# Rounding of the activations on ScalarE, tap sums in PSUM tiles of their own, and a later flag sum in the end of a cross-attention and feed-forward kernel

## The chip, the cores and the metric

The kernel runs on one core of a Trainium2 chip. The time is device microseconds of one execution, as the median of several runs; lower is better. A core has five engines with a queue each, worked in order: TensorE (PE, with its weight loads shown as PEld), VectorE (DVE), ScalarE (ACT), GpSimd (POOL) and SyncE (SP), which mostly issues DMAs. They wait for each other through semaphores.

## The reference

One layer: latents x (2048 x 256) attend to 1601 context rows and to themselves with 4 heads of 64; then comes a feed-forward part with weights rounded to -1, 0, 1 and activations rounded to 8 bits. What matters here is the second part:

```
xq = round(layernorm(x) * 127/max) / (127/max)         # per token
h  = xq @ w1q.T                                        # 256 -> 1024
h  = conv along the tokens, 3 taps, one filter per channel, plus conv_b
h  = silu(h)
hq = round(h * 127/max) / (127/max)                    # per token, max over the 1024 channels
x  = x + hq @ w2q.T                                    # 1024 -> 256
```

## The kernel before

Attention comes first and takes some 590 us: eight units (512 queries x a pair of heads), each with 30 blocks of 128 keys. Scores, an exponential on ScalarE and the product with the values follow each other in a software pipeline; denominators are summed by VectorE and by adding DMAs. It uses an estimate of the row maxima, and a flag (`behind`) says in the end whether the estimate was good enough; only if not, the whole layer is run a second time (`tc.If` in the last lines; this does not happen here).

The feed-forward part works on groups of 256 tokens (8 groups, `NG`), with the 1024 channels as partitions: 8 chunks of 128 channels, two chunks to a "slot", four slots to a group. Groups 0 to 3 are planned into the beats of the attention loop by a table of due times (`plan`, `at`). Group 4's first slot too. The rest runs after the loop: slots 17 to 31 (groups 4 to 7), written out by hand in `tick(i)`, together with the end of attention for the last four blocks of 128 tokens (`head(i)`) and what is left of group 3 (`rest`: its scale rows, its two roundings and its two products, one a tick). All instructions issued through `tensor`, `vector`, `scalar` and `gpsimd` keep the order in which the Python code issues them.

A slot in this last stage goes like this (names as in the profile):

- `hidden`: TensorE, four matmuls into a two-bank PSUM tile `ph` (both chunks, 258 tokens: one more on each side).
- `dequantize`: VectorE multiplies `ph` by the row of token scales `ib_all` into `h` in SBUF.
- first chunk: `end_convolve`, three matmuls with diagonal matrices `dg`, one per tap (six records in the profile), whose sum goes back into the first bank of the slot's `ph`; then ScalarE's Silu with `cb_sb` as bias (`end_silu(s, 0)`) into `t`.
- second chunk: `end_taps`, two ScalarE passes into `pre` and `side`; `end_last_tap`, VectorE adds the third tap into `pre` and GpSimd adds `side`; then Silu (`end_silu(s, 1)`) into `t`.

`t` is 256 tokens x 4 channels of one half group (two slots), with tokens outermost, so a Silu writes one 4-byte value in every 16 bytes.

At the end of a group's slots VectorE takes the maximum over the channels of a half (`magnitudes`, `m`), TensorE transposes it (`tpa`), VectorE makes scales (`am`, `qsc`), GpSimd (ScalarE for the last group) spreads them over a tile `cm`, TensorE transposes that (`tpb`), and ScalarE copies it to `tb`. Then for each half `rounding`: VectorE multiplies `t` by `tb` in place, and rounds by adding and subtracting a large constant (`MAGIC`) in one instruction (line 953), into `hq` in bf16 (one buffer), 4 channels in every 8. `product` is TensorE's eight matmuls `py` per 128 tokens, the first four from half 0 of `hq`, the next four from half 1; two such products make a group. `output` is VectorE's `res` and a DMA to `out` on SyncE's queue; it runs one tick later, ahead of that tick's remaining VectorE work.

[...] In the last stage `ps_1` holds one (transposes), `ph` two tiles of two banks, and `ps_y` three single banks (`dn`, `po`, `py`, `many`). So a `hidden` waits until the Silu of the slot two before has read its sum out of the same tile.

`flag` (line 1134): after the last group's scales VectorE compares the last denominators (`within`, `near`, `worst`), TensorE sums over the partitions (`many`), and VectorE copies the sum to `behind`. TensorE's `tpb` for the last group is issued behind `many`.

Of the kernel before, what the change touches and what calls it, by code (L numbers as in the profile page):

```python
# [10 lines left out]
F32 = mybir.dt.float32  # L11
# [3 lines left out]
AF = mybir.ActivationFunctionType  # L15
ALU = mybir.AluOpType
AX = mybir.AxisListType
PSUM = bass.MemoryType.PSUM

P = 128  # L20
FMAX = 3.4028234663852886e38
MAGIC = 12582912.0
# [7 lines left out]
def layer(  # L30
# [22 lines left out]
    nc = tc.nc  # L53
# [10 lines left out]
    G = 256  # L64
    QPG = G // P
    NG = NL // G
    QW = 512
# [15 lines left out]
    const = ctx.enter_context(tc.tile_pool(name="const", bufs=1))  # L83
# [7 lines left out]
    ones = const.tile([P, P], F32, name="ones")  # L91
    nc.gpsimd.memset(ones, 1.0)
    ones16 = const.tile([P, P], BF16, name="ones16")
    nc.vector.memset(ones16, 1.0)

    neg_half = const.tile([P, 2 * H], F32, name="neg_half")
    nc.gpsimd.memset(neg_half, -0.5)

# [13 lines left out]
    cb_sb = const.tile([P, NH], F32, name="cb_sb")  # L112
# [27 lines left out]
    att = ExitStack()  # L140
# [12 lines left out]
    def big(name):  # L153
        return ps_b.tile([P, 2, 512], F32, tag="big", name=name)
# [19 lines left out]
    tensor, vector = InOrder(nc.tensor), InOrder(nc.vector)  # L174
    scalar, gpsimd = InOrder(nc.scalar), InOrder(nc.gpsimd)
# [108 lines left out]
    with tc.tile_pool(name="pro", bufs=1, side="right") as pro, tc.tile_pool(  # L284
        name="pw", bufs=2, side="right"
# [3 lines left out]
        for a in range(0, NX, 512):  # L289
            n = min(512, NX - a)  # L290
# [338 lines left out]
    with att:  # L629
# [89 lines left out]
        def compare(u, r):  # L719

            if behind is None:
                return
            within = wk.tile([P, QW], BF16, tag="within", name="within")
            vector.tensor_scalar(within, r, math.exp(LAG), None, ALU.is_le)
            vector.scalar_tensor_tensor(within, r, math.exp(-LAG), within, ALU.is_ge, ALU.mult)
            vector.tensor_reduce(near[:, u : u + 1], within, AX.X, ALU.min)
# [72 lines left out]
        for edge in (0, NL + 1):  # L799
# [3 lines left out]
        NC2 = NH // 2  # L803
        groups_ = [{} for _ in range(NG)]
        chunk = {}
        where = {
            "ph": big, "py": lambda: big("py")[:, 0, :D], "later": False,
            "t": lambda: fp.tile([P, G, NC2], F32, tag="t", name="t", bufs=3),
        }
# [12 lines left out]
        def dequantize(s):  # L822
            t0 = s // NP * G
            h = fp.tile([P, 2, G + 2], F32, tag="h", name="h", bufs=2)
            vector.tensor_tensor(
                h, chunk[s]["ph"][:, :, : G + 2],
                ib_all[:, t0 : t0 + G + 2].unsqueeze(1).to_broadcast([P, 2, G + 2]), ALU.mult,
            )
            chunk[s]["h"] = h
# [56 lines left out]

        def end_convolve(s):
            c = s % NP * 2
            for tap in range(3):
                tensor.matmul(  # L890
                    chunk[s]["ph"][:, 0, :G], chunk[c, tap], chunk[s]["h"][:, 0, tap : G + tap],
                    start=(tap == 0), stop=(tap == 2),
                )

        def end_last_tap(s):
            c = s % NP * 2
            h, pre, side = chunk[s]["h"], chunk[s]["pre"], chunk[s]["side"]
            vector.scalar_tensor_tensor(
                pre[:, 1, :], h[:, 1, 2 : G + 2], cw_sb[:, c + 1, 2:3], pre[:, 1, :],
                ALU.mult, ALU.add,  # L900
            )
            gpsimd.tensor_tensor(pre[:, 1, :], pre[:, 1, :], side[:, 1, :], ALU.add)

        def end_silu(s, j):
            g, c = s // NP, s % NP * 2
            if c % NC2 == 0 and j == 0:
                groups_[g].setdefault("t", []).append(where["t"]())
            t = groups_[g]["t"][c // NC2][:, :, c % NC2 + j]
            if j == 0:
                scalar.activation(t, chunk[s]["ph"][:, 0, :G], AF.Silu, bias=cb_sb[:, c : c + 1])  # L910
            else:
                scalar.activation(t, chunk.pop(s)["pre"][:, 1, :], AF.Silu)

# [31 lines left out]
        def rounding(g, i, tokens=slice(0, G)):  # L945
            b = groups_[g]
            t = b["t"][i][:, tokens, :]
            vector.tensor_tensor(
                t, t, b["tb"][:, tokens].unsqueeze(2).to_broadcast(list(t.shape)), ALU.mult
            )  # L950
            if "hq" not in b:
                b["hq"] = fp.tile([P, G, NH], BF16, tag="hq", name="hq", bufs=1)
            vector.tensor_scalar(
                b["hq"][:, tokens, ts(i, NC2)], t, MAGIC, -MAGIC, ALU.add, ALU.add
            )

        def product(g, i):
            b = groups_[g]
            py = b["py", i] = where["py"]()
            for c in range(NH):  # L960
                tensor.matmul(
                    py, b["hq"][:, ts(i, P), c], w2T[:, c, :], start=(c == 0), stop=(c == NH - 1)
                )
# [45 lines left out]
        def unit_beat(k):  # L1009

            u, b = divmod(k, NB)
            return (u, b, beats[b]) if u < len(units) else (u, b, [])
# [11 lines left out]
        for k in range(len(units) * NB):  # L1024
            u, b, blocks = unit_beat(k)
            v, _, following = unit_beat(k + 1)
            g, pr = units[u]
# [49 lines left out]


        loop_ps.close()
        ps_h = att.enter_context(tc.tile_pool(name="ps_h", bufs=2, space=PSUM))  # L1080
        ps_y = att.enter_context(tc.tile_pool(name="ps_y", bufs=3, space=PSUM))

        def y_bank(name):
            return ps_y.tile([P, QW], F32, tag="y", name=name)

        where.update(
            ph=lambda name: ps_h.tile([P, 2, 512], F32, tag="ph", name=name),
            py=lambda: y_bank("py")[:, :D],
            later=True,
            t=lambda: ptp.tile([P, 2, QW], F32, tag="pt", name="t").rearrange(  # L1090
                "p h q -> p (h q)"
            ).rearrange("p (t c) -> p t c", c=NC2),
# [22 lines left out]
        def run(sub, *names):  # L1115
            for n in names:
                steps[sub][n]()
# [16 lines left out]
        def flag():  # L1134

            compare(len(units) - 1, r)
            if behind is None:
                return
            worst = sm.tile([P, 1], F32, tag="worst", name="worst")
            vector.tensor_reduce(worst, near, AX.X, ALU.min)  # L1140
            vector.tensor_scalar(worst, worst, 0.5, None, ALU.is_lt)
            many = y_bank("many")[:, :1]
            tensor.matmul(many, ones, worst, start=True, stop=True)
            vector.tensor_copy(behind, many)

        rest = [call for key in sorted(plan) for call in plan.pop(key)]
        slots = list(range(4 * NP + 1, NG * NP))
        N = len(slots)

        def tick(i):  # L1150

            at_ = {i - ((g - 4) * NP - 1) + (g == NG - 1): g for g in range(4, NG)}
            if 0 <= i - 2 < N:
                end_silu(slots[i - 2], 1)
            if 0 <= i - 1 < N:
                end_silu(slots[i - 1], 0)
            if i < N:
                dequantize(slots[i])
            if i >= N and 0 <= i - 1 < N:
                end_last_tap(slots[i - 1])  # L1160
            if 6 in at_:
                magnitudes(at_[6], 1)
                columns(at_[6])
            while outputs:
                output(*outputs.pop(0))
            if 0 <= i - 1 < N and i < N:
                end_last_tap(slots[i - 1])
            if i < N:
                end_taps(slots[i])
            if 6 in at_:  # L1170
                scales(at_[6], at_[6] == NG - 1)
                if at_[6] == NG - 1:
                    flag()
            if 7 in at_ and at_[7] != NG - 1:
                scales_spread(at_[7])
                rounding(at_[7], 0)
            if 8 in at_ and at_[8] != NG - 1:
                rounding(at_[8], 1)
            if 4 in at_:
                magnitudes(at_[4], 0)  # L1180
            if 7 in at_ and at_[7] == NG - 1:
                g = at_[7]
                scales_spread(g, True)
                for n in range(QPG):
                    for half in range(2):
                        rounding(g, half, ts(n, P))
                    product(g, n)
                for n in range(QPG):
                    output(g, n)
            if i + 1 < N:  # L1190
                hidden(slots[i + 1])
            if i < N:
                end_convolve(slots[i])
            if 1 <= i <= NSUB:
                run(i - 1, TURN)
            if 8 in at_ and at_[8] != NG - 1:
                for n in range(QPG):
                    end_product(at_[8], n)
# [54 lines left out]
```

## Time and profile before

| | us |
|---|---|
| median of 3 runs | 688.37 (687.83 to 688.69) |
| the profiled execution | 688.55 |
| its span, first to last instruction | 686.7 |
| TensorE busy | 629.2 (92%) |
| VectorE busy | 464.1 (68%) |
| ScalarE busy | 423.8 (62%) |
| GpSimd busy | 276.6 (40%) |
| last row of VectorE (res) starts | 681.89 |

The profile is of one execution. Rows of the timeline show the start within the span, the duration, the engine and operation, the output and inputs, and in brackets how long the engine had been idle and who ended it. Most instructions are recorded in a helper, so that all have the line of that helper (L170), and one goes by tile names. The granted clock is the share of full speed that TensorE was given; over the whole span it is 0.972, and all that is missing is missing in the last 70 us.

### The profile page before, as it was taken

How to read it: one execution, taken by the hardware profiler on the slowest of the kernel's cores; microseconds unless marked ns; L12 is line 12 of the kernel's file. 1: busy time of each engine (PE TensorE's matmuls, PEld its weight loads, DVE VectorE, ACT ScalarE, POOL GpSimd, SP SyncE). 2: the span in 40 equal slices, each digit the busy share in tenths (PEclk: the TensorE clock that was granted, in tenths of full speed). 3: DMA queues.
4: the chain of work that ended last, by engine and by line, in shares of the span. 5: the costliest groups of instructions: out<-in, count | busy, mean ns of one | idle time of the engine just before them, and what ended most of it. 6: DMA issues, size and time to landing. Idle time of an engine off the chain costs nothing. (4 is left out here: it accounts for less than half of the span.)

```text
span 686.7 us, 8000 instructions
## 1 busy us (share of the span) xinstructions
PE 629.2 (92%) x2796; PEld 266.3 (39%) x2796; DVE 464.1 (68%) x770; ACT 423.8 (62%) x535; POOL 276.6 (40%) x331
## 2 busy tenths in 40 slices
PE   4999898999999999999999999998899999857754
PEld 2555563333333333333334333332333333345542
DVE  3658774332832766596378779757966797897885
ACT  1656556554556445669945469998765789545540
POOL 2656673221221234244245433425354446742330
PEclk9999999999999999999999999999999999997975
DMA  7600003685878674478849447693564576100001
GB/s 241 170 0 0 1 1 92 128 161 111 167 140 183 128 148 93 93 154 152 185 96 172 101 107 154 125 182 94 107 123 92 132 138 114 31 0 16 16 16 36
DMA packets 32220, 72.12 MB, mean 105 GB/s; under 512 B 7531, under 2 KB 16940, under 8 KB 32172
## 3 DMA queue, kind: packets, MB, share of 16 engines
q0 software_dynamic: 16560, 60.30, 43.3%
q1 hardware_dynamic: 14524, 10.45, 5.1%
q10 hardware_dynamic: 1088, 0.79, 0.4%
q8 instruction: 24, 0.39, 0.2%
q14 instruction: 24, 0.20, 0.1%
HBM read 9.13 MB, written 2.10 MB: 16 GB/s over the span
## 5 line engine op out<-in xcount | busy, mean ns | idle before, releaser
L170 ACT ACTIVATE pt<-st,bias 128x1024 f32<-128x1024 f32 x232 | 242.8, 1112 | 123.1 <-issue 64.6
L170 PE MATMUL st<-q_un,kT 64*128 64x512 f32 x928 | 223.7, 611 | 4.7 <-DVE res L170 1.8
L170 PE MATMUL ot<-pt,v_sb 128*64 128x512 f32 x928 | 216.6, 600 | 0.0
L170 DVE TENSOR_TENSOR vec<-vec,pt 128x1024 f32<-128x1024 f32 x107 | 136.7, 1278 | 40.2 <-ACT pt L170 36.3
L170 PEld LDWEIGHTS st<-q_un,kT 64*128 64x128 f32 x928 | 83.0, 187 | 124.8 <-issue 91.3
L170 PEld LDWEIGHTS ot<-pt,v_sb 128*64 128x64 f32 x928 | 60.2, 136 | 136.7 <-issue 130.4
L170 POOL DMA_DIRECT2D acd<-pt x54 | 44.9, 831 | 127.9 <-ACT pt L170 61.4
L170 POOL DMA_DIRECT2D acc<-pt x61 | 52.7, 865 | 69.4 <-ACT pt L170 51.7
L170 POOL TENSOR_TENSOR pre<-pre,side 128x512 f32<-128x512 f32 (+1 forms) x32 | 38.3, 1196 | 62.3 <-DVE pre L170 51.4
L170 ACT ACT_TABLE_LOAD x34 | 43.6, 1283 | 16.6 <-DMA lb<-in_L_xattn_ln_l_b_dram 7.4
L170 PE MATMUL kv<-wkv_sb,feat 128*128 128x512 f32 (+1 forms) x116 | 52.9, 599 | 0.0
L170 POOL TENSOR_TENSOR ss<-ss,neg_half 128x8 f32<-128x8 f32 (+1 forms) x23 | 39.1, 1702 | 1.9
L170 ACT ACTIVATE t<-pre 128x512 f32<-128x512 f32 (+1 forms) x32 | 29.7, 928 | 11.8 <-POOL pre L170 11.6
L170 POOL TENSOR_SCALAR cm<-ones,units 128x128 f32<-128x128 f32 x16 | 11.8, 739 | 61.4 <-DVE units L170 57.9
L170 DVE COPY oT<-ot 128x512 f32<-128x512 f32 x8 | 5.5, 691 | 44.6 <-PE ot L170 44.6
L170 DVE TENSOR_REDUCE ss<-sq 128x8 f32<-128x512 f32 (+1 forms) x23 | 15.5, 672 | 29.0 <-ACT sq L170 28.9
L170 DVE TENSOR_TENSOR h<-ph,ib_all 128x516 f32<-128x516 f32 x32 | 21.9, 686 | 19.0 <-PE ph L170 18.6
L170 PE MATMUL ph<-h,dg 128*128 128x256 f32 x90 | 25.8, 428 | 7.4 <-DVE h L170 7.4
L170 DVE RECIPROCAL r<-dn 128x512 f32<-128x512 f32 (+1 forms) x11 | 27.3, 2478 | 5.7 <-PE dn L170 5.7
L170 PEld LDWEIGHTS kv<-wkv_sb,feat 128*128 128x128 f32 (+1 forms) x116 | 21.2, 192 | 21.9 <-issue 20.9
L170 ACT ACTIVATE side<-h,cw_sb 128x256 f32<-128x256 f32 x66 | 29.6, 506 | 0.0
L170 PE MATMUL py<-w2T,hq 128*128 128x256 bf16 x128 | 20.8, 317 | 7.2 <-DVE hq L170 7.2
(129 smaller groups left out, 708.9 us busy)
## 6 DMA issues: line engine op xcount, KB each, us to landing
acc<-pt POOLq DMA_DIRECT2D x61, 512.0 KB, 5.1
acd<-pt POOLq DMA_DIRECT2D x54, 512.0 KB, 4.8
tok<-in_x_dram SPq DMA_DIRECT2D x4, 512.0 KB, 6.1
w_sb<-in_L_ffn_w_dram SPq DMA_DIRECT2D x4, 512.0 KB, 5.3
q_un<-in_x_dram SPq DMA_DIRECT2D x4, 512.0 KB, 3.9
out_dram<-res SPq DMA_DIRECT2D x16, 128.0 KB, 1.7
tok<-in_ctx_dram SPq DMA_DIRECT2D x3, 512.0 KB, 4.7
wkv_sb<-in_L_xattn_W_kv_dram ACTq DMA_DIRECT2D x1, 512.0 KB, 7.2
```

Source lines behind the costliest of these rows:

```text
L170: return tc.keep_in_program_order(getattr(self.engine, name)(*args, **kwargs))
```

## The change

Three edits, all in the last stage, besides a constant tile.

1. The sum of the three taps goes to a PSUM tile of its own, `cv` (one bank, two of them), in place of the slot's `ph`. To make room, there is one `ph` tile in place of two.
2. For groups other than the last, in this stage, ScalarE does the rounding: two passes (Identity with a bias column of plus and minus `MAGIC`), the first in place in `t`, the second from `t` into `hq`. VectorE still does the multiply with `tb`. This is for groups 3, 4, 5 and 6, two halves each.
3. The sum of the flag over the partitions and its copy (`spread_flag`) are issued after the first of the last group's four roundings. The comparisons stay where they were.

On each engine's queue this means: TensorE has the same instructions in the same order, but for `many`, which now comes behind the last `tpb`; the first `ph` matmul of a slot waits for VectorE in place of ScalarE, and the `py` matmuls of four groups for ScalarE in place of VectorE. VectorE has eight instructions less and two memsets more. ScalarE has sixteen more: in a steady group a pair behind the copy to `tb`, then two Silus and the next slot's `pre` and `side`, then the second pair. GpSimd and SyncE have no change.

```
+    magic = const.tile([P, 2], F32, name="magic")
+    nc.vector.memset(magic[:, 0:1], MAGIC)
+    nc.vector.memset(magic[:, 1:2], -MAGIC)
...
         def end_convolve(s):
             c = s % NP * 2
+            chunk[s]["cv"] = where["cv"]()
             for tap in range(3):
                 tensor.matmul(
-                    chunk[s]["ph"][:, 0, :G], chunk[c, tap], chunk[s]["h"][:, 0, tap : G + tap],
+                    chunk[s]["cv"], chunk[c, tap], chunk[s]["h"][:, 0, tap : G + tap],
                     start=(tap == 0), stop=(tap == 2),
                 )
...
-                scalar.activation(t, chunk[s]["ph"][:, 0, :G], AF.Silu, bias=cb_sb[:, c : c + 1])
+                scalar.activation(t, chunk[s]["cv"], AF.Silu, bias=cb_sb[:, c : c + 1])
...
-            vector.tensor_scalar(
-                b["hq"][:, tokens, ts(i, NC2)], t, MAGIC, -MAGIC, ALU.add, ALU.add
-            )
+            hq = b["hq"][:, tokens, ts(i, NC2)]
+            if where["later"] and g < NG - 1:
+                scalar.activation(t, t, AF.Identity, bias=magic[:, 0:1])
+                scalar.activation(hq, t, AF.Identity, bias=magic[:, 1:2])
+            else:
+                vector.tensor_scalar(hq, t, MAGIC, -MAGIC, ALU.add, ALU.add)
...
-        ps_h = att.enter_context(tc.tile_pool(name="ps_h", bufs=2, space=PSUM))
+        ps_h = att.enter_context(tc.tile_pool(name="ps_h", bufs=1, space=PSUM))
+        ps_c = att.enter_context(tc.tile_pool(name="ps_c", bufs=2, space=PSUM))
...
+            cv=lambda: ps_c.tile([P, QW], F32, tag="cv", name="cv")[:, :G],
...
             vector.tensor_scalar(worst, worst, 0.5, None, ALU.is_lt)
+            held["worst"] = worst
+
+        def spread_flag():
             many = y_bank("many")[:, :1]
-            tensor.matmul(many, ones, worst, start=True, stop=True)
+            tensor.matmul(many, ones, held["worst"], start=True, stop=True)
             vector.tensor_copy(behind, many)
...
                     for half in range(2):
                         rounding(g, half, ts(n, P))
+                        if (n, half) == (0, 0) and behind is not None:
+                            spread_flag()
                     product(g, n)
```

More of the change, by code (lines that the diff above doesn't have):

```diff
@@ L1141, in flag @@
             vector.tensor_scalar(worst, worst, 0.5, None, ALU.is_lt)
+            held["worst"] = worst
+        def spread_flag():
             many = y_bank("many")[:, :1]
-            tensor.matmul(many, ones, worst, start=True, stop=True)
+            tensor.matmul(many, ones, held["worst"], start=True, stop=True)
             vector.tensor_copy(behind, many)
+        held = {}
         rest = [call for key in sorted(plan) for call in plan.pop(key)]
```

## The prediction

> **What bounds the kernel now.** First the table of stages, busy time of each engine in stretches of the span (columns: stretch, length, then PE, weight loads, DVE, ACT, POOL, granted clock, DMA share, GB/s).
>
> ```profile
> 14.00:590.00 576.00, 563.69 (x2488) 221.98 (x2489) 380.98 (x586) 382.28 (x456) 242.46 (x274) 1.00 0.56 117
> 590.00:626.00 36.00, 23.36 (x105) 13.72 (x102) 31.32 (x73) 13.77 (x27) 15.53 (x24) 0.89 0.01 4
> 626.00:672.00 46.00, 33.03 (x178) 25.18 (x175) 37.80 (x62) 24.34 (x48) 14.61 (x17) 0.87 0.06 20
> ```
>
> Up to 590 us TensorE is busy 98% of the time and the diff touches nothing there that runs. Everything changed runs in the last 96 us, where VectorE is the fullest engine (31.3 of 36, 37.8 of 46) and ScalarE about half full. So the question is the order in VectorE's queue. Its timeline through group 5, with the two roundings, and the same stretch of TensorE:
>
> ```profile
> 647.40 1.22 DVE L170 TENSOR_TENSOR t<-t,tb 128x1024 f32<-128x1024 f32 x1 [1.29 <-ACT tb L170]
> 648.66 0.69 DVE L170 TENSOR_SCALAR hq<-t 128x1024 bf16<-128x1024 f32 x1
> ...
> 650.27 1.22 DVE L170 TENSOR_TENSOR t<-t,tb 128x1024 f32<-128x1024 f32 x1
> 651.52 1.11 DVE L170 TENSOR_SCALAR hq<-t 128x1024 bf16<-128x1024 f32 x1
> 652.55 1.21 DVE L170 TENSOR_REDUCE m<-t 128x256 f32<-128x1024 f32 x1
> 653.68 0.68 DVE L170 TENSOR_TENSOR h<-ph,ib_all 128x516 f32<-128x516 f32 x1
> 654.28 0.86 DVE L170 SCALAR_TENSOR_TENSOR res<-py,am,q_un 128x256 f32<-128x256 f32 x2
> 655.06 0.47 DVE L170 SCALAR_TENSOR_TENSOR pre<-h,cw_sb,pre 128x256 f32<-128x256 f32 x1
> ```
>
> ```profile
> 651.41 0.60 PE L170 MATMUL py<-w2T,hq 128*128 128x256 bf16 x4
> 652.69 1.53 PE L170 MATMUL py<-w2T,hq 128*128 128x256 bf16 x12 [0.67 <-DVE hq L170]
> 654.06 0.60 PE L170 MATMUL ph<-xq_all,w1T 128*128 128x258 bf16 x4
> ```
>
> VectorE has no hole from 647.40 to 655.06, 7.66 us. But see how near the loop through TensorE is: the product's last twelve matmuls start when the second hq is rounded, end at 654.22, and the second of the two res at 654.28 (it starts at about 654.67) needs the last of them. If the rounding is over 0.5 us late, VectorE stands still at res, in order, and behind it wait the next h, the last maximum m and through it the next group's scales. The only waits of a group are that of 1.29 us for tb (a chain DVE, POOL, PE, ACT, DVE) and 0.13 for tpa, and both lie after res, so they can't take up a delay of res.
>
> **Part 1, the roundings (line 953).** Four groups (3 to 6) lose two VectorE instructions each: in steady state slots of 0.61 and 1.03 us (start to start above; the second is long because POOL's pre sum runs against it, 1.58 us there and 0.73 elsewhere). That is 1.64 a group, 6.5 in all. ScalarE gets two passes for each, four a group: t plus the constant, in place, then minus the constant into hq. No row has that shape. Rows by shape:
>
> ```profile
> L170 ACT ACTIVATE pt<-st,bias 128x1024 f32<-128x1024 f32 x232 | 242.8, 1112 | 123.1 <-issue 64.6 <-PE st L170 43.8 <-DMA acc<-pt 7.7
> L170 ACT ACTIVATE side<-h,cw_sb 128x256 f32<-128x256 f32 x66 | 29.6, 506 | 0.0
> L170 ACT ACTIVATE t<-pre 128x512 f32<-128x512 f32 x17 | 19.5, 1150 | 0.2
> L170 ACT ACTIVATE t<-pre 128x256 f32<-128x256 f32 x15 | 10.2, 677 | 11.6 <-POOL pre L170 11.6
> ```
>
> The nearest is the exponential with its bias column, 1.11 us for 1024 elements. The second pass waits for the first, so a pair is 1.11 + 0.03 + 1.11 = 2.25 us until hq is readable, 2.16 of ScalarE's queue. [...] 0.69 us against 2.25, so the move pays only where ScalarE's time is hidden. [...] by the rows it is a matter of what waits behind the pair.
>
> The second pass writes strided: four bf16, 8 bytes, in every 16. The Silu rows write one f32 in every 16 bytes, and cost (1150 - 677)/256 = 1.85 ns an element, against 0.83 or so that side and pt imply ((1112 - 506)/768 = 0.79). Taking the Silu row as the price of a stride, the second pass is 0.2 + 1024 x 1.85 = 2.1 us. [...] I take 1.11, since VectorE writes the same pattern in 0.69 us, faster than its contiguous t multiply of as many elements (1.22); 2.1 is kept for the range. [...]
>
> ScalarE's queue then reads, per group: tb, pair of half 0, Silu, Silu, pre, side (one tick), pair of half 1. Half 1 is multiplied by VectorE early but its pair stands behind those. From the start of the first t multiply in a steady group: multiply and wake 1.27; pair 2.16; Silu 0.46 + Silu 0.47 + pre 0.46 + side 0.40 (back-to-back starts at 656.44 to 657.83) = 1.79; second pair 2.25: hq ready at 7.47. TensorE wakes and does four matmuls (0.06 + 0.60), so res of the first half starts at 8.17; twelve matmuls take 1.53, so the second starts at 7.53 + 1.53 + 0.04 = 9.10 and leaves its slot (0.40) at 9.50. Before: 7.66. So +1.85 for group 5, the same for group 4. VectorE's saved 1.64 is already inside this: it turns into a hole of some 3 us ahead of res.
>
> Group 6 (last, no h left in between): the first t starts at 662.90, the second res6 at 671.51, 8.61 us. After: 1.27 + 2.16 + two Silus 0.93 + 2.25 = 6.61, then twelve matmuls at the half clock of that stretch (0.06 + 2.79 in the timeline at 668.70) = 9.46, and res at 9.50: +0.9. The last Silu, behind the second pair, lets the last m start at 7.23 in place of 5.93; m, its join and the first res are done by 9.22, so this is covered by the matmuls, barely.
>
> Group 3: its roundings fall among the final blocks' norms, where VectorE is full from 609 to 622 us: -1.02 (hq at 612.33) and -0.61 (619.70), pairs hidden behind the next product at 626.27. I take -1.6 and give part of it back in part 2.
>
> **Part 2, the sums of taps in two tiles of their own, one ph tile (lines 893 and 1080).** Same 45 matmuls. The ph product of the next slot no longer waits for ScalarE's Silu two slots back (TensorE waits 5.6 us for that in this stage, five times), but for VectorE's h of the slot before: h to h is at least 0.69 + 0.06 + 0.60 = 1.35. VectorE's own h are 1.2 to 6 us apart, mostly over 3: nothing in the steady state, and the waits it removes were off the path, since TensorE is idle about a third of the stage. At two places it costs: at tick 1 the po matmuls go behind ph and the taps, some 0.4 us later with res q_un behind them; and at 621 the ph product runs after h rather than ahead of it, with the taps, yq turns and product behind it on the path (VectorE waits 2.35 us at 628.23): 0.45 warm, 0.9 at half clock. Together +1.2 or so. Group 3 with this: -1.6 + 1.2 = -0.4.
>
> **Part 3, the flag's sum later.**
>
> ```profile
> 672.80 0.23 DVE L170 TENSOR_SCALAR am<-am,w_mean 128x2 f32<-128x2 f32 x1
> 675.03 0.15 DVE L170 TENSOR_SCALAR worst<-worst 128x1 f32<-128x1 f32 x1
> 675.87 0.16 DVE L170 CAST behind<-many 128x1 int32<-128x1 f32 x1 [0.68 <-PE many L170]
> 676.40 0.69 DVE L170 TENSOR_TENSOR t<-t,tpb 128x512 f32<-128x512 f32 x1 [0.37 <-PE tpb L170]
> ```
>
> Now tpb runs ahead of many: cm is ready at 673.5, tpb at 674.2, and the multiply starts when VectorE is through the comparison, 675.2: -1.2. The copy comes back behind the first rounding: +0.15, -1.05 net. SyncE's load of the flag (474 ns, its queue's last two stores behind it) then starts near 1.2 us after that multiply, 3 us before res is there: nothing. The two memsets (0.06 us each, as second at 0.92) lie under the 4.33 us wait for the first tokens: nothing.
>
> **Part 4, the clock.** In steady groups TensorE now has nothing from the product's first four matmuls (done near 4.1 of the count above) to 7.53, a hole of 3.4 us. Such holes are followed by half clock here:
>
> ```profile
> 612.48:615.89 3.41, 0.73 (x6) 0.28 (x3) 3.20 (x10) 1.57 (x4) 0.68 (x2) 1.00 0.00 0
> 619.30:622.72 3.42, 1.12 (x5) 0.40 (x3) 3.14 (x10) 1.58 (x4) 0.08 (x1) 0.50 0.00 0
> ```
>
> The twelve matmuls behind it are then 2.79 in place of 1.53. From none to both groups 4 and 5: 0 to 2.5; I take one, +1.25.
>
> **Sum.** -0.4 + 1.85 + 1.85 + 0.9 - 1.05 + 1.25 = +4.4. The profiled execution took 688.55 (span 686.7 and 1.85 around it), 0.2 above the median of 688.37; the difference goes on the median: **692.8 us**.
>
> **Rivals.** (a) *ScalarE is hidden*: VectorE keeps its 1.64 a group, 688.4 - 6.5 - 1.05 = 680.8. For it: ScalarE is half idle, the removed instructions are on the full engine. Against: res needs hq. It decides only if the second rounding is ready 1.8 us after its multiply starts (2.35 now, plus 0.44 of slack, less the 1.03 by which res would come sooner); a pair alone takes 2.25, and four activations stand ahead of it: 5%. (b) *TensorE stays at full clock*, the other side for the same chain: minus the 1.25, and minus what half clock costs now on the path (taps at 623.12 2.93 against 1.53, the product at 626.27 1.91 against 1.04, the tb wait of group 6 2.21 against 1.29, res6 and the end about 1.2): 4.4. 692.8 - 1.25 - 4.4 = 687.1, no change or a little faster. [...] the new holes speak against it: 9%. (c) *Half clock through most of the stage*: both holes and the taps behind them, +2.5 to 3: 695.5, 12%. (d) *Strided second pass at the Silu price*: 0.98 more a pair, two pairs on the path in groups 4, 5 and 6: +5.9, 698.7, 12%. The chain as summed: 62%, by itself 690.8 to 694.8.
>
> **Chances and range.** A difference under 0.2% (1.4 us) can't be told from none. Faster: (a) and 4 of (b)'s 9: 0.09; same: the rest of (b): 0.05; slower 0.86. Range 689.5 to 699.0: leaves out (a), (b) and tails of some 5%.
>
> **What would show it.** Group 5's VectorE row res with a wait of about 3 us for PE py; PE py waiting for ACT hq; no PE ph waiting for ACT t; ACT rows hq and t 128x1024 at 1.11 each; first t to next first t of a group near 16.5 us against 14.96 and 15.50 now; the multiply of the last group 0.1 us after worst, not 1.4. The prediction is wrong if res has no wait, if the hq pass takes 2 us, or if the granted clock in the last 70 us is all 1.00.

## The result

The changed kernel takes **691.67 us** (median of 7 runs, 689.26 to 692.57) against 688.37 (median of 7, 686.78 to 688.69): a ratio of **1.0048, 95% interval 1.0029 to 1.0067**, so +3.3 us (2.0 to 4.6). The prediction was 692.8, +4.4, with a range of 689.5 to 699.0.

The profiled execution took 689.39 (span 687.5), 2.3 us less than the median. Executions of this kernel fall into 689.3 and 691.6 to 692.6, and the profile is one of the shorter ones; where those 2.3 us may lie is said in the section on what was not expected. So the profile is read here by the distance between rows, and not by its total.

The table of stages of the changed kernel (stretch, length, then PE, weight loads, DVE, ACT, POOL, granted clock, DMA share, GB/s):

```profile
14.00:590.00 576.00, 563.66 (x2494) 221.65 (x2492) 382.56 (x588) 383.63 (x457) 243.66 (x275) 1.00 0.56 117
590.00:626.00 36.00, 23.13 (x121) 15.66 (x118) 30.55 (x74) 18.69 (x37) 15.08 (x24) 0.95 0.01 4
626.00:672.00 46.00, 28.99 (x149) 21.32 (x148) 28.82 (x48) 33.10 (x55) 14.86 (x16) 0.87 0.05 15
```

From 626 to 672 us VectorE is busy for 28.8 us in place of 37.8, and ScalarE for 33.1 in place of 24.3: the work moved as the diff says. No engine is full in that stretch any more, and yet less of the kernel fits into it: the stage is bound by waiting. Three of the longest in the table of waits from 590 to 690 us, by who waits for what (total, times, longest), show where:

```profile
PE ph L174 <- DVE h L174: 11.9, 7, 3.4
PE py L174 <- ACT hq L174: 11.6, 4, 3.4
DVE res L174 <- PE py L174: 11.2, 7, 3.7
```

Before, in the same stretch, `py` did not wait for ScalarE and res waited 3.9 in total, at most 2.4 at once. Group 5's rows in the timeline show the second and the third, one behind the other:

```profile
646.19 1.23 DVE L174 TENSOR_TENSOR t<-t,tb 128x1024 f32<-128x1024 f32 x1 [1.29 <-ACT tb L174]
...
652.65 1.15 ACT L174 ACTIVATE hq<-t,magic 128x1024 bf16<-128x1024 f32 x1
653.85 2.78 PE L174 MATMUL py<-w2T,hq 128*128 128x256 bf16 x12 [3.36 <-ACT hq L174]
654.96 0.48 DVE L174 SCALAR_TENSOR_TENSOR res<-py,am,q_un 128x256 f32<-128x256 f32 x1 [3.69 <-PE py L174]
656.67 0.48 DVE L174 SCALAR_TENSOR_TENSOR res<-py,am,q_un 128x256 f32<-128x256 f32 x1 [1.22 <-PE py L174]
```

ScalarE ends the second half's rounding at 653.8; TensorE has stood for 3.36 us and takes 2.78 for twelve matmuls (1.53 before; from 653.24 to 656.66 the granted clock is 0.50, in the kernel before it is 1.00 from 628.40 to 655.71); VectorE stands at res for 3.69 and again for 1.22, where before it had no hole there. The chain that ended last (start, us, what) runs through exactly these pieces:

```profile
646.19 1.24 DVE t L174
647.45 1.16 ACT t L174
648.63 1.15 ACT hq L174
649.77 1.05 ACT t L174 x2
650.82 0.36 ACT pre L174
651.18 0.40 ACT side L174
651.58 1.05 ACT t L174
652.65 1.16 ACT hq L174
653.85 2.79 PE py L174 x12
656.70 0.37 issue
657.07 0.48 DVE pre L174
```

From the first multiply of the group to the instruction behind res it is 657.07 - 646.19 = 10.88 us, against 7.66 before. ScalarE's two passes, by shape (count | busy, mean ns | idle before):

```profile
L174 ACT ACTIVATE hq<-t,magic 128x1024 bf16<-128x1024 f32 x8 | 9.2, 1149 | 0.3
L174 ACT ACTIVATE t<-t,magic 128x1024 f32<-128x1024 f32 x8 | 9.1, 1143 | 3.9 <-DVE t L174 3.9
```

And the flag's part in VectorE's queue at the end:

```profile
677.07 0.15 DVE L174 TENSOR_SCALAR worst<-worst 128x1 f32<-128x1 f32 x1
677.18 0.69 DVE L174 TENSOR_TENSOR t<-t,tpb 128x512 f32<-128x512 f32 x1
...
678.24 0.15 DVE L174 CAST behind<-many 128x1 int32<-128x1 f32 x1
```

The multiply starts 0.11 us after `worst` starts (1.37 before), and the copy is behind the first rounding.

### The profile page after: what moved, and what is told of

Read it like the earlier page. It is cut to its first block, busy times and chain, and to the rows that moved or that the text cites. A ratio compares the mean times of both kernels' runs of the same rounds, so it can differ in the third digit from the quotient of the medians.

```text
span 687.5 us, 8009 instructions
## 1 busy us (share of the span) xinstructions
PE 627.1 (91%) x2796; PEld 265.5 (39%) x2796; DVE 457.6 (67%) x764; ACT 438.8 (64%) x551; POOL 277.6 (40%) x331
## 5 line engine op out<-in xcount | busy, mean ns | idle before, releaser
L174 PE MATMUL py<-w2T,hq 128*128 128x256 bf16 x128 | 22.9, 340 | 12.2 <-ACT hq L174 11.6
L174 PE MATMUL ph<-xq_all,w1T 128*128 128x258 bf16 x128 | 20.2, 281 | 12.8 <-DVE h L174 11.9
```

What stands on the lines that cost most here:

```text
L174: return tc.keep_in_program_order(getattr(self.engine, name)(*args, **kwargs))
```

## The experiments

All kernels were timed beside the kernel before on the same chip, whose median was 687.1 to 687.3 there; differences in us are (ratio - 1) x 687.2, with the 95% interval. The changed kernel's own +3.3 is from its own comparison, where the kernel before had 688.37; so differences between rows of this table are taken between ratios, with an interval made of both.

| kernel | ScalarE rounds | tiles | flag | ratio (95%) | us |
|---|---|---|---|---|---|
| the change | groups 3 to 6, both halves | own | later | 1.0048 (1.0029 to 1.0067) | +3.3 |
| e1 | groups 3 to 6, both halves | shared | as before | 1.0103 (1.0077 to 1.0129) | +7.1 |
| e10 | groups 3 to 6, both halves | own | as before | 1.0069 (1.0047 to 1.0091) | +4.7 |
| e2 | groups 3 to 6, half 0 | own | later | 0.9949 (0.9930 to 0.9967) | -3.5 |
| e8 | groups 3 to 6, half 0 | shared | later | 1.0011 (0.9999 to 1.0024) | +0.8 |
| e11 | group 3, both halves | own | later | 0.9951 (0.9933 to 0.9969) | -3.4 |
| e7 | none | own | later | 0.9970 (0.9961 to 0.9979) | -2.1 |
| e5 | none | own | as before | 1.0000 (0.9991 to 1.0009) | 0.0 |
| e6 | none | shared | later | 0.9993 (0.9985 to 1.0001) | -0.5 |
| e3 | as the change, product a tick later | own | later | 0.9983 (0.9972 to 0.9995) | -1.2 |
| e4 | as the change, more matmuls | own | later | 1.0029 (1.0012 to 1.0046) | +2.0 |
| e9 | as e2, more matmuls | own | later | 0.9952 (0.9939 to 0.9965) | -3.3 |

### What res waits for: e2, half 0 alone on ScalarE

```
-            if where["later"] and g < NG - 1:
+            if where["later"] and g < NG - 1 and i == 0:
                 scalar.activation(t, t, AF.Identity, bias=magic[:, 0:1])
                 scalar.activation(hq, t, AF.Identity, bias=magic[:, 1:2])
```

> As the changed kernel, but ScalarE rounds only half 0 of the four groups; VectorE rounds half 1 as before. Theory (the second pair, behind four queued activations, is what res waits for): the first pair is ready at about 3.5 us after its multiply, before TensorE reaches the product, so no wait of res for the product over 1 us, VectorE keeps 0.61 us in each of groups 4 to 6 and the flag's 1.05 us: 688.4 - 1.8 - 1.05 = 685.5. Rival (any rounding on ScalarE costs, because the Silus behind it come late and hold the maxima, or because TensorE falls to half clock anyway): 690 or more.

Measured: 683.61 us (682.16 to 684.84), ratio 0.9949 (0.9930 to 0.9967). The second pair is gone from ScalarE's queue, VectorE rounds half 1 itself, and the same rows of group 5 are:

```profile
650.47 1.53 PE L174 MATMUL py<-w2T,hq 128*128 128x256 bf16 x12 [0.26 <-DVE hq L174]
652.07 0.86 DVE L174 SCALAR_TENSOR_TENSOR res<-py,am,q_un 128x256 f32<-128x256 f32 x2
```

res has no wait, the twelve matmuls take 1.53 us in place of 2.78, and the groups follow each other every 14.08 and 13.86 us (first multiplies at 631.83, 645.91, 659.77) in place of 17.79 and 17.80 in the changed kernel (628.40, 646.19, 663.99). So it is the second pair, behind the first pair, two Silus, `pre` and `side`, that the group waits for; the first pair is hidden. This version beats the kernel before and the changed one. But against e7 below, which has the same tiles and flag and rounds everything on VectorE, it is only -1.4 us (-2.9 to 0.0): most of its -3.5 comes from the other two edits.

### Is it only the place of the product: e3, product one tick later

```
-            if 8 in at_ and at_[8] != NG - 1:
+            if 9 in at_ and at_[9] != NG - 1:
                 for n in range(QPG):
-                    end_product(at_[8], n)
+                    end_product(at_[9], n)
```

> As the changed kernel, both halves on ScalarE, but the product of groups 4 to 6 is issued one tick later, behind that tick's ph and taps on TensorE, and so its res one tick later on VectorE. Theory (the loss is where the product stands in the queues, not ScalarE's work): res waits under 1 us, VectorE keeps most of 1.64 us a group, 688.4 - 0.4 - 3 x 1.64 - 1.05 = 682, up to 686 if half clock takes some of it. Rival (ScalarE itself is the bound, or late Silus hold the maxima): 690 or more, with VectorE's m waiting for ACT t in groups 4 and 5.

Measured: 686.57 us (683.61 to 687.09), ratio 0.9983 (0.9972 to 0.9995), a little faster than before, but less so than was expected. The stall at res is gone, but not all of it is won. Group 4's rows on VectorE:

```profile
639.55 1.22 DVE L174 TENSOR_REDUCE m<-t 128x256 f32<-128x1024 f32 x1 [1.67 <-ACT t L174]
641.14 0.87 DVE L174 SCALAR_TENSOR_TENSOR res<-py,am,q_un 128x256 f32<-128x256 f32 x2
```

Now the maximum `m` waits 1.67 us for ScalarE's Silu, which stands behind the second pair: of the 4.89 us that VectorE stood at the two res of this group (3.67 and 1.22), 1.67 have gone to the next reader of ScalarE's queue. The periods are 14.84 and 14.62, where e11, which rounds these groups on VectorE, has 14.98 and 14.58: the 1.64 us of VectorE's work that a group is rid of buy nothing. In group 6 something is lost as well: its last maximum waits 3.38 us, its two res come between `worst` and the last group's first multiply, and from group 6's first multiply to that one it is 13.75 us in place of 12.25 in e11. Four passes more in a group's share of ScalarE's queue are late for one reader or another.

### The clock: e4, more matmuls in the holes

```
             py = b["py", i] = where["py"]()
+            if where["later"] and 3 < g < NG - 1 and i == 0:
+                for _ in range(6):
+                    for c in range(NC2):
+                        tensor.matmul(
+                            py, b["hq"][:, ts(i, P), c], w2T[:, c, :], start=(c == 0), stop=(c == NC2 - 1)
+                        )
```

> As the changed kernel, with the first four matmuls of the product of the first 128 tokens issued six more times ahead of it in groups 4 to 6 (their result is overwritten), which puts some 2.8 us of TensorE work into its hole of 3.4 us. Theory (the hole costs because the clock falls to half in it): the twelve matmuls behind it take 1.5 in place of 2.8 us in groups 4 and 5, waits of the two res 3.4 and 0.1 us in place of 3.7 and 1.2: 691.7 - 2.5 = 689.2. Rival (the clock does not depend on this hole, or full clock gains nothing on the path): 691.7 or a little more.

Measured: 688.91 us (686.81 to 690.45), ratio 1.0029 (1.0012 to 1.0046). TensorE does 24 matmuls more in each of three groups, and in group 4:

```profile
632.09 3.27 PE L174 MATMUL py<-w2T,hq 128*128 128x256 bf16 x28
636.13 1.53 PE L174 MATMUL py<-w2T,hq 128*128 128x256 bf16 x12 [0.77 <-ACT hq L174]
```

The twelve matmuls behind them take 1.53 in place of 2.78, the second res waits 0.39 in place of 1.22, and the periods are 16.59 and 16.58 in place of 17.79 and 17.80. In the changed kernel the granted clock is 0.50 behind the holes of both groups (636.18 to 639.59, 653.24 to 656.66); in e4 it is 1.00 from 628 to 647.5 us, and group 5's twelve take 1.53 as well. So half clock costs 1.2 us in each of groups 4 and 5 of the changed kernel, and with the hole filled it did not occur. (A hole doesn't bring it every time: see group 4 of e10 in the last section.) In total that is -1.3 us against the changed kernel by the two ratios, with an interval of about 1.8 on each side: in place the effect is plain, in the total it is not told from none.

### The rounding without the tiles: e1, and e8 for half 0

e1 undoes the tiles and the flag:

```
-            chunk[s]["cv"] = where["cv"]()
+            chunk[s]["cv"] = chunk[s]["ph"][:, 0, :G]
...
-        ps_h = att.enter_context(tc.tile_pool(name="ps_h", bufs=1, space=PSUM))
-        ps_c = att.enter_context(tc.tile_pool(name="ps_c", bufs=2, space=PSUM))
+        ps_h = att.enter_context(tc.tile_pool(name="ps_h", bufs=2, space=PSUM))
...
             held["worst"] = worst
+            spread_flag()
...
-                        if (n, half) == (0, 0) and behind is not None:
-                            spread_flag()
```

> Only the rounding is moved to ScalarE; the tap sums stay in the slot's ph tile (two tiles) and the flag's sum stays where it was. By the prediction's steps the tiles alone cost about +1.2 us and the flag's move alone gains 1.05, so against the changed kernel's 691.7 this gives 691.7 - 1.2 + 1.05 = 691.5. Rival: with the sums in ph a ph tile comes free only after ScalarE's Silu, which now stands behind a rounding pair of 2.3 us, so that TensorE's ph products and VectorE's h are held up in each of the groups 4 and 5 and in group 3: 2 us or more for each, 695 to 698. Then the tiles of their own are what keeps the rounding from costing more.

Measured: 693.20 us (692.91 to 695.48), ratio 1.0103 (1.0077 to 1.0129), +7.1 (5.3 to 8.9). The expectations were counted from 688.4: +3.1 by the steps, +6.6 or more by the rival. The rival holds; in the profile `ph` waits six times for ScalarE's Silu, 16.0 us in all, against 5.6 before. The result is 3.4 parts in a thousand over e10, which differs from it in the tiles alone: with both halves on ScalarE the tiles save 2.3 us, with an interval as wide as that (0 to 4.7). With half 0 alone on ScalarE it is clearer. e8 is e2 with the first two pieces of the diff above:

> ScalarE rounds half 0 only, flag later, but the tap sums stay in the shared ph tiles. Theory A (the prediction's sign for the tiles): they cost 1.2, so this is 1.2 faster than half 0 with tiles of their own, which was 3.5 below before: 682.6, ratio 0.993. Theory B (from the run with the rounding alone): with ScalarE busy with a pair, its Silu of the first chunk is late, and with shared tiles the ph product waits for that Silu, then h, the taps and the maximum: the tiles then save several us, and this kernel is slower than before, some 690 to 692, ratio 1.004 to 1.007, with PE ph waiting for ACT t over 2 us in groups 4 and 5.

Measured: 688.11 us (686.08 to 690.89), ratio 1.0011 (0.9999 to 1.0024); theory A's 0.993 is outside, theory B's 1.004 to 1.007 is missed too, but by less and on the side of its sign. The tiles are worth 0.0062, 4.3 us (2.7 to 5.8), beside a ScalarE that rounds. Where they save is seen in TensorE's rows of group 5 in e8:

```profile
651.79 1.02 PE L174 MATMUL ph<-xq_all,w1T 128*128 128x258 bf16 x4 [3.44 <-ACT t L174]
...
652.60 2.49 PE L174 MATMUL ph<-h,dg 128*128 128x256 f32 x6
...
654.92 1.91 PE L174 MATMUL py<-w2T,hq 128*128 128x256 bf16 x16
```

With shared tiles the next slot's `ph` product waits for a Silu that stands behind the pair; TensorE takes the taps and all sixteen matmuls of the product behind that `ph`, as they were issued. With tiles of their own there is no such wait (the changed kernel's table of waits has `ph` waiting for VectorE's h, and for no Silu), and the first four matmuls of the product run as soon as half 0 is rounded.

### The tiles alone, the flag alone, both

e5 is the change with VectorE's rounding everywhere and the flag in its old place, e6 the flag alone, e7 tiles and flag. The edit that all three share:

```
-            if where["later"] and g < NG - 1:
+            if False:
                 scalar.activation(t, t, AF.Identity, bias=magic[:, 0:1])
                 scalar.activation(hq, t, AF.Identity, bias=magic[:, 1:2])
```

> Only the tile part of the change: tap sums in two tiles of their own, one ph tile; VectorE rounds everything, the flag's sum where it was. The prediction put this part at +1.2 us (po 0.4 later behind ph and the taps at the start of the last stage, the ph product of slot 22 behind h for 0.45 to 0.9): the time is then 688.4 to 688.9 beside 687.3 before, ratio 1.0017. A rival says that the tiles cost next to nothing as long as VectorE rounds (the waits for ScalarE's Silu were off the path, and so are the new ones for h): within 0.5 us of before, ratio 0.9993 to 1.0007, with the period from first t to first t unchanged at 15.0 to 15.5 us. In neither does it save much alone, whatever it is worth beside the rounding on ScalarE.

Measured: 686.77 us (685.71 to 688.89), ratio 1.0000 (0.9991 to 1.0009). The rival's zero is right, the step's +1.2 is outside.

> Only the flag's sum later. The prediction's step is -1.2 at the last group's first multiply and +0.15 for the copy behind the first rounding, -1.05: ratio 0.9985. A rival says that the later sum saves more than its step, since tiles and flag together came to -2.1 (0.997) and the tiles alone to nothing: 0.997. In the trace the first multiply of the last group starts 0.1 us after the comparison in both; the rival needs a further gain ahead of it or behind it, before the last res.

Measured: 686.85 us (685.42 to 687.59), ratio 0.9993 (0.9985 to 1.0001). The step's -1.05 is at the edge of the interval, the rival's -2.1 outside.

> The tiles and the later flag sum, VectorE rounding everything: the change without its ScalarE part. By the prediction's steps +1.2 - 1.05 = +0.15, so no difference that can be told (ratio 1.000). If the tiles cost nothing, -1.05: 686.2, ratio 0.9985. Against the changed kernel, 3.3 above before, this makes the ScalarE part alone worth some +3.2 to +4.3. In the trace the last group's first multiply starts 0.1 us after the flag's comparison.

Measured: 685.25 us (684.26 to 687.35), ratio 0.9970 (0.9961 to 0.9979): faster than either expectation. Zero and -0.5 add up to -0.5 (-1.3 to 0.3), and -2.1 (-2.7 to -1.4) lies beyond that. From `worst` to the last res it is 6.86 us before and in e5, 5.26 in e6 and 5.47 in e7, so the flag's part is 1.4 to 1.6 in these traces, with the clock of the last matmuls in it; in the changed kernel, whose last res waits 0.78 us as before, it is 5.66, 1.20 less. One place where the tiles give something back is seen in two rows, the scale wait of group 6 in e6 and in e7:

```profile
662.91 1.23 DVE L174 TENSOR_TENSOR t<-t,tb 128x1024 f32<-128x1024 f32 x1 [2.15 <-ACT tb L174]
```

```profile
662.85 1.23 DVE L174 TENSOR_TENSOR t<-t,tb 128x1024 f32<-128x1024 f32 x1 [1.29 <-ACT tb L174]
```

With shared tiles this wait is 2.15 (2.21 before), with own tiles 1.29: the taps that TensorE runs ahead of `tpb` meet half clock in the one (granted 0.81 from 658 to 660 us and 0.50 from 660 to 662 in e6) and full clock in the other (1.00 from 652 to 666 in e7). A difference stands a little earlier: with own tiles the `ph` product waits 0.19 us for h and the taps follow it later, so that TensorE's hole ahead of `tpa` is 1.69 us in place of 2.03. The last section sets such holes beside the clock.

### Which groups: e11, group 3 alone, and e10, no flag

```
-            if where["later"] and g < NG - 1:
+            if where["later"] and g == 3:
```

> The changed kernel with ScalarE's rounding for group 3 alone; VectorE rounds groups 4 to 6. Against tiles and flag without any rounding on ScalarE (0.997): by the prediction's step -1.6, ratio 0.9947. A rival says that what VectorE saves among the norms is lost in waiting for the same end of attention (TensorE's po and VectorE's h), so nothing: 0.997. The rest of the changed kernel's +5.4 to +7 then lies in groups 4 to 6, where the steps put 1.85 + 1.85 + 0.9 + 1.25 = 5.85.

Measured: 684.68 us (681.82 to 685.86), ratio 0.9951 (0.9933 to 0.9969). Against e7 that is -1.3 us (-2.7 to +0.1), with the step's -1.6 in the interval and 0 just in it. In the traces group 3's first multiply to group 4's is 20.57 us (611.06 to 631.63) against 21.79 in e7 (611.70 to 633.49), -1.2; but e5, which up to there is the same program as e7, has 19.30 (611.80 to 631.10), so the traces can't confirm it. Against e11 the changed kernel is +6.7 us (4.9 to 8.5) by rounding groups 4 to 6 on ScalarE as well.

e10 moves `spread_flag` back ahead of the roundings, as the last pieces of e1's diff:

> The changed kernel without its flag part: tiles and ScalarE's rounding of both halves. If the parts add, 3.3 plus 1.05 (the step) to 2.1 (as tiles and flag together came to): +4.4 to +5.4 over before, ratio 1.0063 to 1.0078. If the flag part is worth nothing beside the rounding, ratio 1.0048 as the changed kernel.

Measured: 692.85 us (689.24 to 693.55), ratio 1.0069 (1.0047 to 1.0091). The flag is worth 1.4 us (-0.6 to 3.4) beside the rounding: as it should be if the parts add, though nothing at all isn't excluded.

### Is there more to gain: e9, e2 with TensorE kept busy

```
+        def warm(out, n):
+            for _ in range(n):
+                tensor.matmul(out, ones16, w2T[:, 0, :], start=True, stop=True)
...
             py = b["py", i] = where["py"]()
+            if where["later"] and 3 < g < NG - 1 and i == 0:
+                warm(py, 14)
...
-            many = y_bank("many")[:, :1]
+            many = y_bank("many")[:, :D]
+            warm(many, 14)
+            many = many[:, :1]
```

> ScalarE rounds half 0 only (with tiles and flag as changed), and TensorE gets 14 more 128x256 products of a constant ahead of the product of groups 4 to 6 and 14 ahead of the flag's sum, so that it doesn't stand idle there; their sums are overwritten. If the clock falls because of those holes and is on the path: the last twelve matmuls of group 6 take 1.5 in place of 2.78 (-0.6 to -1.2 at the second res), the sixteen of group 7 2.1 to 2.6 in place of 4.31, of which some 0.8 shows at the last res: 1.4 to 2 below half 0 alone (3.5 below before), so ratio 0.992 to 0.993. If the half clock is hidden behind VectorE's roundings: as half 0 alone, ratio 0.995. If the added matmuls delay tpb's readers or hq's: slower than half 0 alone.

Measured: 684.67 us (682.49 to 684.75), ratio 0.9952 (0.9939 to 0.9965), as e2 alone. In group 6 the last twelve matmuls do take 1.53 in place of 2.78, and the second res is read some 0.7 us sooner. But in groups 4 and 5 the added matmuls stand in front of the product: the second res waits 0.39 us there, none in e2, and the periods are 14.63 and 14.41 us in place of 14.08 and 13.86, 1.1 lost in all. The end doesn't gain either. From the last group's first multiply to the last res e2 and e9 both have 5.56 us, since VectorE's roundings pace the first eight of the sixteen matmuls, and the last eight take 2.13 us, where eight took 1.04 before at full clock (630.15):

```profile
673.71 2.13 PE L174 MATMUL py<-w2T,hq 128*128 128x256 bf16 x8 [0.40 <-DVE hq L174]
```

So the matmuls pay in group 6, where e2's twelve take 2.78 (granted clock 0.50 from 665 to 667), and cost 0.55 us a group in groups 4 and 5, where e2's take 1.53; both sizes are below what the intervals of these two runs can tell.

## Why the prediction was right, step by step

**The bound and the mechanism.** Right: VectorE's saved time turned into a hole ahead of res, res waits for `py`, `py` for the second rounding on ScalarE. e2 takes that pair away and the stall goes with it.

**The length of a pass.** 1.11 us was taken, 1.149 and 1.143 were measured; a pair is 2.33 us (647.45 to 649.78) against 2.25. Rival (d), 2.1 us for the strided pass, is excluded by the row. The pass writes four values in every 16 bytes, in 1.149 us. The Silu row, one value in every 16 bytes, was the wrong neighbour; whether its price is that of the stride or of the function, no run separates. That a pair on ScalarE takes longer than VectorE's rounding (2.33 us against 0.69) shows in groups 4 to 6 taken together, +6.7, but not in each pair: in e2 the first pairs of the four groups are hidden, and the kernel is no slower than e7 (-1.4, -2.9 to 0.0).

**+1.85 for group 5, and as much for group 4.** The twelve matmuls behind the second pair start at 653.85 - 646.19 = 7.66 (predicted 7.53), and the instruction behind res at 10.88, where 9.50 and 1.25 for half clock make 10.75. With the clock held by more matmuls (e4) the period is 16.59, about the 16.5 that was named; against e11, the same kernel with these groups on VectorE (14.98 and 14.58), it is +1.6 and +2.0. The term is right.

**+1.25 for the clock, one hole of two.** Both groups have the hole and half clock behind it (2.76 and 2.78 us) in the changed kernel's profile; in e10, the same program up to the flag, only group 5 has it (res waits 3.68 and 1.22 there, 3.27 and 0.39 in group 4). So it was rightly "none to both", and which of them differs between executions; that one of two came near the measured time is in part luck, as nothing shown decided for one. The two stretches that the prediction showed are not the ones that count: the clock stayed at 1.00 for 2.3 us after the first of them, until 618.16, and the second lies wholly in a time at half clock (618.16 to 628.40). The stretch behind which it fell is the one from 614.75 to 618.16, with 1.21 us of TensorE work.

**+0.9 for group 6.** First multiply to second res: 673.58 - 663.99 = 9.59, against 8.61: +0.98. Here the maximum waits 3.45 us for ScalarE, as in the working, and ends just ahead of the matmuls (the second res still waits 0.19 for `py`).

Together groups 4 to 6 were put at 1.85 + 1.85 + 0.9 + 1.25 = 5.85; e11 and the change measure +6.7 (4.9 to 8.5).

**-1.6 for group 3.** -1.3 (-2.7 to 0.1) measured by e11 against e7: in line with the step, and not clear of zero.

**+1.2 for the tiles.** This is the step that failed. It held that there was "nothing in the steady state, and the waits it removes were off the path", and charged 1.2 us for two places in the head. e5 measures 0.0 (-0.6 to 0.6), and the traces show a gain that was left out: the scale wait of group 6 falls from 2.2 to 1.29 us, with the taps there at full clock (1.00 in e7, 0.81 and 0.50 in e6); the period from group 5 to group 6 is 14.57 or 14.58 in e5, e7 and e11, and 15.44 to 15.50 with shared tiles. The prediction had that very wait among what half clock costs now, and did not see that the tile edit would take it away. Whether the 1.2 in the head is there and paid back by this, or was never there, can't be read off: the same program differs there by 2.5 us between the profiles of e5 and e7. Beyond that the step was costed with VectorE's roundings in mind: with ScalarE rounding, shared tiles make `ph` wait for ScalarE, and own tiles then save 2.3 us (0 to 4.7) with both halves moved and 4.3 with one.

**-1.05 for the flag.** The multiply comes 1.26 sooner after `worst`, and the copy behind the first rounding, as written. Alone it measured -0.5 (-1.0 to 0.1), on top of the rounding -1.4, on top of the tiles -2.1. In the changed kernel's trace the part from `worst` to the last res is 1.20 shorter. The step is in line with that and with the first two (at the edge of the first); why tiles and flag together gain more than their sum is open.

**The sum.** By e5, e7, e11 and the change, one after the other: 0.0 - 2.1 - 1.3 + 6.7 = +3.3. The prediction had +1.2 - 1.05 - 1.6 + 5.85 = +4.4. Its surplus of 1.1 is about what the tiles were overcharged; that the flag (-2.1 for -1.05, on top of the tiles) and the rounding (+5.4 for +4.25) then err by as much in opposite ways is luck. In another order, e5, e10 and the change, it is 0.0 + 4.7 - 1.4, and flag and rounding are nearer to their steps. Each of these differences is uncertain by one to two us, and the total's own interval, 2.0 to 4.6, reaches 4.4.

**The rivals.** (a) falls: ScalarE isn't hidden for both halves, though it is for one. (b) falls: the granted clock was 0.95 and 0.87 in the two stretches from 590 to 672 us. (c) has both holes in the profiled execution, but that execution is of the shorter kind, with less half clock in the head than e10, and no execution reached 695.5. (d) falls by the row.

## What to carry to other kernels

Work moved to an engine with idle time is free only as long as its reader comes later than that engine's queue: add up the queue in order, from the input's arrival to the reader, and not the engine's busy share. Here the first of two pairs fitted in front of its reader and the second, behind four other activations, did not, so against the same kernel with all rounding on VectorE (e7) moving half changed the time by -1.4 us (-2.9 to 0.0), and moving all by +5.4 (3.9 to 6.8). Value two edits together as well as one by one: the tiles are worth nothing alone, and 4.3 us where ScalarE also rounds half.

## What was not expected of the hardware

**Where the half clock falls isn't fixed by the program.** Up to the flag e10 and the changed kernel are the same program. From group 3's first multiply to group 4's the profiled executions take 20.57 us (610.80 to 631.37) and 18.25 (610.15 to 628.40). The first row of the last stage in e10's table, same columns as above, has a granted clock of 0.78:

```profile
590.00:626.00 36.00, 24.86 (x100) 16.63 (x101) 27.78 (x68) 16.00 (x32) 13.39 (x22) 0.78 0.00 0
```

It is 0.95 in the changed kernel's row above. The difference, 2.3 us, is as much as the profiled execution lies below its median; that it is the same 2.3 us isn't shown, as no longer execution of the changed kernel was profiled. In return group 4 is at full clock in e10 (period 16.87) and at half clock behind its hole in the changed kernel (17.79).

**The changes of the clock lay multiples of 3.41 us apart.** In the profiles of the kernel before and of the changed one all changes between full and half clock, from 590 us to the last instruction, lie whole multiples of 3.413 us apart, to within 0.01 us; in those of e1 to e4 so do all from 600 to 647.5 us. (Not all half clock lies in the last 70 us: before, the clock is also 0.50 from 495.28 to 498.69, 36 times 3.413 us ahead of 618.16.) A beat is such a length of 3.413 us here. In the changed kernel the stretches behind the holes of groups 4 and 5 are at half clock from 636.18 to 639.59 and from 653.24 to 656.66, 17.07 us apart, five beats. Group 4's hole is 3.36 us in the changed kernel and in e10; in the one it fills a beat, and in the other two beats share it (same columns; first the changed kernel, then e10):

```profile
632.76:636.18 3.42, 0.12 (x1) 0.12 (x2) 0.73 (x2) 3.39 (x6) 0.00 (x0) 1.00 0.00 0
636.18:639.59 3.41, 3.41 (x17) 2.68 (x18) 1.21 (x3) 1.62 (x4) 0.00 (x0) 0.50 0.11 38
```

```profile
634.01:637.42 3.41, 1.98 (x12) 1.37 (x10) 2.76 (x3) 3.38 (x7) 1.59 (x1) 1.00 0.01 2
637.42:640.83 3.41, 1.48 (x14) 1.46 (x15) 0.48 (x1) 3.38 (x6) 0.00 (x0) 1.00 0.00 0
```

With 0.12 us of work the next beat is at half clock; with 1.98 the next is at full clock. Counted over the profiles of the kernel before and of the changed one (beats that begin between 593 and 676 us): of 36 at full clock, eight were followed by half clock and had 0.12 to 1.56 us of work, and the other 28 had 1.40 to 3.40. Of 12 at half clock, the six that full clock followed had 2.81 us or more, and the other six 0.66 to 2.54.

Group 6's scale wait, where VectorE rounds, can be set beside this. A stretch of 3.41 us laid over the hole ahead of `tpa` holds at least 1.71 us of work with own tiles (e7), and down to 1.38 with shared ones (before, e6). In the profile before one beat lies so, from 655.71 to 659.12 with 1.38 us, and the next is at 0.50; in e7 the clock is 1.00 from 652 to 666. That own tiles keep full clock there in every execution is not shown. A difference of one or two us between two profiles says little of an edit, unless the beats are laid over both: the 2.3 us above came without one.

**More work can be faster.** 24 matmuls more in a hole of TensorE made each of groups 4 and 5 1.2 us shorter (e4).

**A strided pass can be as cheap as a contiguous one.** ScalarE's pass into hq, four bf16 in every 16 bytes, takes 1149 ns, and the contiguous one in f32 over the same number of elements 1143 (the two differ in output type as well). Silu with one f32 in every 16 bytes takes 1148 for half as many; what of that is the stride and what the function isn't separated.
